# A transformer block on one core: what the last token tile of each batch does before attention starts, and where two small pieces of work stand

## Chip, cores and metric

The kernel runs on one core of one Trainium2 chip. Its time is in device microseconds; the figure for a kernel is the median of its runs. The kernel before has three runs: 3191.1, 3191.3 and 3192.64 us, so its median is 3191.3 us. One more execution was profiled. All times of instructions come from that one execution and count from the start of its span.

## The reference, cut to what matters

The block takes two sequences of 2048 tokens with 576 features (B = 2, N = 2048, C = 576, 16 heads of 36 features).

```
mod = silu(c) @ w_ada + b_ada                       # six rows of 576 per batch
xn  = layernorm(x) * (1 + sc_msa) + sh_msa
q, k, v = split((xn @ w_qkv + b_qkv) by head)       # 576 -> 1728
q = layernorm(q per head) * qn_g + qn_b
k = layernorm(k per head) * kn_g + kn_b
o = softmax(q @ k.T * 36**-0.5) @ v                 # per batch and head, 2048 x 2048 scores
x = x + g_msa * (o @ w_proj + b_proj)
h = gelu((layernorm(x) * (1 + sc_mlp) + sh_mlp) @ w1 + b1)   # 576 -> 2304
x = x + g_mlp * (h @ w2 + b2)                       # 2304 -> 576
```

All tensors are float32.

## The kernel before

A branch on the size of the gains and biases picks `block_of_small`, the only branch of interest. It goes through six stages in this order: for batch 0 the products q, k, v (`inputs`), attention (`attend`) and the output projection (`outputs`); the same three for batch 1; then the first product of the MLP for eight blocks of 512 tokens, and the second product.

**`inputs`.** The tokens of a batch are cut into 16 tiles of 128 (t = 0 to 15). For each tile TensorE makes three products (`product`, L1085 for the four full chunks of features and L1087 for the last 64). Each fills one tile of PSUM named `s`, two banks large, of which there are four in rotation. DVE adds the bias on the way out of PSUM (`biased`: L1099 for q and k into `both`, L1102 for v into `vt`). Then, for q and k, ACT squares (`squared`), DVE sums the squares by head, ACT takes the root, DVE the reciprocal, and POOL multiplies (`head_scale`, L1043, L1046, L1048, L1050). `by_feature` (L1063, L1065) transposes a tile in squares of 32 on DVE into one of two buffers `turned_qk`, and four DMAs on SP's queue store it by feature in a tensor `qk` in DRAM. Rows of one head pair are read back from there by `take_k_block` and `take_q` (L812, L814, SP's queue) for the first head pair, and by `take_k` (POOL's queue) for the other seven. The 36 features of a head are split: 32 go to `km` or `qm`, 4 to `ke` or `qe`, each of these four repeated. The rows then get their gain and bias on DVE and the four last features are split into two parts of a product in float32r (`scaled`, `parted`: L843 twice, L852, L853). For a block of key rows these four DVE instructions are the function `made` that `take_k_block` returns.

`key_tiles` lists where the key rows of the first head pair are cut into blocks: after tiles 4, 8, 12, 14 and 16. When `by_feature` has stored the tile that ends a block, it issues that block's loads and puts `made` in the list `taken`; the next call of `by_feature` with `ready=True` runs what is in the list, after its own transpose and stores. What is left in the list at the end of the stage is handed to attention, which runs it in its second step (hook (0, 0, 0) puts it in front of the list for step 1).

The loop over t from 0 to 14 has the same order for every tile; the last tile, t = 15, has its own sequence, which is what most of the change is about. Once in batch 0 `gains_by_row` turns gains and biases into one number per row of `km`, `ke`, `qm`, `qe` (`gb_at`): DVE fills two selection matrices (L824, L829), TensorE multiplies them with the gains (L835), DVE copies the result out (L838). `kept` stores the prepared weights in DRAM for batch 1. Both are called in the iteration t = 2.

**`attend`.** A step is one head pair, one block of 512 queries and a quarter of the keys. TensorE makes the scores of the step (`scores`, L1203, eight banks of PSUM), ACT takes exponentials (L1207), and in the next step TensorE multiplies the exponentials of the step before with v (`values`, L1216), and DVE adds the result to `ot` (L1264, L1266). The column range of `km` that a step reads is a quarter g of its 1024 columns; its rows 0 to 63 hold tokens 0 to 1023 and rows 64 to 127 tokens 1024 to 2047. So step g = 2 reads tiles 4, 5, 12 and 13, and step g = 3 reads 6, 7, 14 and 15. The eight banks `b` lie where the four tiles `s` of `inputs` were, and a bank can be written once the `s` tile in its place has left PSUM.

**The first product of the MLP.** 144 jobs alternate between two sets of banks. A job has its matmuls (L1625, L1639) and then `gelu_stored`: ACT copies one bank (L1651), DVE combines seven products into four (L1652 to L1659), ACT takes gelu (L1663). Beside them `ahead` prepares the next block of tokens, tile by tile: load from `x1_dram` (`mlp_loaded`, POOL's queue), normalise and transpose on DVE (`tile_turned`), store, read back, modulate on ACT. The first two loads, for tiles 1 and 2 of block 1, are issued before the first job, ahead of `token_sums(0)` in the text of the program.

**What sets the order.** PE runs in the order of the text throughout, and DVE in the order of the text in all stages that matter here; in attention ACT and POOL do too. The order of the other queues is set by a scheduler, from what it takes each instruction to wait for. It had put the two first loads of the MLP, which need only rows of batch 0, into POOL's queue at the last tile of batch 1, between the multiplications of `head_scale`.

Of the kernel before, what the change touches and what calls it, by code (L numbers as in the profile page):

```python
# [31 lines left out]
def dit_block(  # L32
# [25 lines left out]
    nc = tc.nc  # L58
# [9 lines left out]
    TPB = BLK // P  # L68
# [54 lines left out]
    def halves(ap):  # L123
        return ap.rearrange("p (a f) -> p a f", a=2)
# [627 lines left out]
    def block_of_small():  # L752
# [3 lines left out]
        xs = {}  # L756
# [114 lines left out]
        def take_k_block(t0, t1):  # L871

            c, k0 = divmod(t0 * P, N // 2)
            dst, rows = slice(k0, k0 + (t1 - t0) * P), slice(64 * c, 64 * c + 64)
            rows_taken(nc.sync, km[0], ke[0], (c,), C, lambda c: slice(t0 * P, t1 * P), dst)

            def made():
                scaled(km[0][rows, dst], km[0][rows, dst], rows, 1)
                parted(ke[0][:, dst], rows, 1)

            return made

        def take_q(p, qb):
            i, full = qb % 2, slice(0, P)
            src = lambda c: slice(qb * BLK, (qb + 1) * BLK)
            rows_taken(nc.sync, qm[i], qe[i], range(2), p * 2 * HD, src, slice(0, BLK))
            return [lambda: scaled(qm[i], qm[i], full, 0), lambda: parted(qe[i], full, 0)]
# [140 lines left out]
        def inputs(b, weights, making, work, xnts, turned, loaded):  # L1028

            wq, wq4, bq = weights  # L1030
            both, squares, taken = {}, {}, []
            key_tiles = (0, 4, 8, 12, 14, 16)

            def squared(t, w0=0, w1=2):
                if squares.get("t") != t:
                    squares.update(t=t, sq=work.tile([P, 2 * C], F32, name="sq", bufs=1))
                part = slice(w0 * C, w1 * C)
                nc.scalar.activation(squares["sq"][:, part], both[t][:, part], AF.Square)

            def head_scale(t, w0=0, w1=2):  # L1040
                n, part = (w1 - w0) * H, slice(w0 * C, w1 * C)
                var = work.tile([P, 2 * H], F32, name="var", bufs=2)[:, :n]
                nc.vector.tensor_reduce(  # L1043
                    var, squares["sq"][:, part].rearrange("p (h d) -> p h d", d=HD), AX.X, ALU.add
                )
                nc.scalar.activation(var, var, AF.Sqrt, bias=eps5, scale=1.0 / HD)  # L1046
                inv = work.tile([P, 2 * H], F32, name="inv", bufs=2)[:, :n]
                nc.vector.reciprocal(inv, var)  # L1048
                heads = both[t][:, part].rearrange("p (h d) -> p h d", d=HD)
                nc.gpsimd.tensor_tensor(heads, heads, inv.unsqueeze(2).to_broadcast([P, n, HD]), ALU.mult)  # L1050
# [5 lines left out]
            def by_feature(t, w0=0, w1=2, ready=True):  # L1056

                begun = [*taken] if ready else []
                if ready:
                    taken.clear()  # L1060
                part = slice(w0 * C, w1 * C)
                turned_qk = work.tile([P, 2 * C], F32, name="turned_qk", bufs=2)
                nc.vector.transpose(turned_qk[:, part], both[t][:, part])  # L1063
                for g in range(P // SQ):
                    nc.sync.dma_start(  # L1065
                        out=by_square[t, g][:, w0 * NSQ : w1 * NSQ, :],
                        in_=turned_qk[g * SQ : (g + 1) * SQ, part].rearrange("p (k j) -> p k j", j=SQ),
                    )
                for do in begun:
                    do()  # L1070
                if t == TPB - 1 and w0 == 0:
                    taken.extend(take_q(0, 0))
                if t + 1 in key_tiles and w1 == 2:
                    i = key_tiles.index(t + 1)
                    taken.append(take_k_block(*key_tiles[i - 1 : i + 1]))
# [18 lines left out]
            def biased(w, ps, t):  # L1094
                bias = halves(bq[:, w * C : (w + 1) * C])
                if w < 2:
                    if t not in both:
                        both[t] = work.tile([P, 2 * C], F32, name="both", bufs=4)
                    nc.vector.tensor_tensor(halves(both[t][:, w * C : (w + 1) * C]), ps[:, :, :HALF], bias, ALU.add)  # L1099
                else:  # L1100
                    heads = "p a (h d) -> p a h d"
                    nc.vector.tensor_tensor(  # L1102
                        vv[:, t, :, 0:HD].rearrange("p (a h) d -> p a h d", a=2),
                        ps[:, :, :HALF].rearrange(heads, d=HD),
                        bias.rearrange(heads, d=HD),
                        ALU.add,
                    )
# [37 lines left out]
            for t in range(NT - 1):  # L1145
                begun(t)
                if t >= done:
                    q = product(0, t)
                k = product(1, t)
                if t >= done:  # L1150
                    biased(0, q, t)
                turned_ahead(t)
                biased(1, k, t)
                if t > 0:
                    head_scale(t - 1)
                if t >= done:
                    v = product(2, t)
                    biased(2, v, t)
                if b == 0 and t == 2:
                    gains_by_row(work)  # L1160
                    kept()
                if t >= 2:
                    by_feature(t - 2)
                squared(t)
                modulated_ahead(t)

            t = NT - 1
# [2 lines left out]
            by_feature(t - 2)  # L1170
            biased(1, k, t)
            squared(t, 1, 2)
            by_feature(t - 1)
            head_scale(t, 1, 2)
            by_feature(t, 1, 2)
            biased(0, q, t)
            squared(t, 0, 1)
            biased(2, v, t)
            head_scale(t, 0, 1)
            by_feature(t, 0, 1, ready=False)  # L1180
# [359 lines left out]
        for j in range(TPB + 1):  # L1540
            n, t = divmod(j, TPB)
# [15 lines left out]
        def mlp_loaded(n, i, queue):  # L1557
            b, blk = divmod(n, NBLK)
            t0 = blk * BLK + i * P
            return tile_loaded(x1_dram[b, t0 : t0 + P, :], queue)  # L1560
# [31 lines left out]
        def token_sums(n):  # L1592
            a = xnts[n % 2][0]
            a00, a01, a10, a11 = (a[:, 2 * k : 2 * k + 2, t * PAIR : (t + 1) * PAIR] for t in range(2) for k in range(2))
            nc.vector.tensor_tensor(ss[1], a10, a11, ALU.add)
            nc.vector.tensor_tensor(ss[2], ss[1], a00, ALU.subtract)
            nc.vector.tensor_tensor(a10, a00, a10, ALU.subtract)
            nc.vector.tensor_tensor(ss[4], a01, ss[2], ALU.subtract)
# [107 lines left out]
            nc.sync.dma_start(out=hidden[q % len(hidden)], in_=gelus[n][g])  # L1706

        rows_ahead = {}
        for i in (1, 2):
            rows_ahead[1, i] = mlp_loaded(1, i, nc.gpsimd)  # L1710
        token_sums(0)
        for job in range(0, NB * HF, 2):
            (n0, f0), (n1, f1) = divmod(job, HF), divmod(job + 1, HF)
            ahead(job)
# [157 lines left out]
```

## Time and profile before

| what | value |
|---|---|
| median of the three runs | 3191.3 us |
| the profiled execution: its own time | 3187.14 us |
| its span, first to last instruction | 3185.4 us |
| TensorE busy | 3122.8 us, 98% of the span |
| DVE, ACT, POOL busy | 48%, 46%, 21% |
| mean granted TensorE clock | 0.992 |

The profile lists for each engine when it was busy, and for the time before an instruction in which its engine was idle, what released it ("<-"). TensorE's matmuls are pipelined and their ends are modelled. An idle engine costs time only where the engine that sets the end waits for it. Here that is TensorE almost everywhere: between 2193 and 2690 us, the middle of the first MLP product, it is busy for 497.00 of 497.00 us.

### The profile page before, as it was taken

The page shows a single profiled execution, that of the slowest core. Times are in us where ns is not written, and L with a number is a line of the kernel's source. Part 1 is how long each engine was busy: PE and PEld are TensorE (multiplying, and loading weights), DVE is VectorE, ACT ScalarE, POOL GpSimd, SP SyncE. Part 2 cuts the span into 40 slices and gives each one's busy share as a digit, 9 for nine tenths or more (in the row PEclk, how much of TensorE's full clock was granted, in tenths as well). Part 3 has the DMA queues.
Part 4 walks back from the last instruction along what each step waited for, and adds up shares of the span by engine and source line. Part 5 has one row for each costly group of instructions (what it writes and reads, how often), then busy time and mean ns, then how long its engine had stood idle before and what let it go on. Part 6 is the DMA issues. An engine that isn't in the chain of part 4 may idle for free.

```text
span 3185.4 us, 46758 instructions
## 1 busy us (share of the span) xinstructions
PE 3122.8 (98%) x17553; PEld 1865.6 (59%) x17553; DVE 1518.5 (48%) x2182; ACT 1471.6 (46%) x2843; POOL 658.1 (21%) x921
## 2 busy tenths in 40 slices
PE   7998999999999999899999999999999999999999
PEld 5873333333333787633333333358888888777777
DVE  6653344433434555434434444346566554455454
ACT  2225666666666122266666666642555552000000
POOL 4551000111110455300001111113333320121121
PEclk9998999999999999899999999999999999999999
DMA  6554211222221756511122222246554433333331
GB/s 187 115 108 97 76 45 56 67 74 67 73 73 41 213 112 118 97 39 46 46 49 69 81 64 68 65 139 189 155 144 131 138 108 143 124 126 112 119 104 38
DMA packets 304454, 311.94 MB, mean 98 GB/s; under 512 B 183450, under 2 KB 237466, under 8 KB 302107
## 3 DMA queue, kind: packets, MB, share of 16 engines
q1 hardware_dynamic: 256834, 193.37, 21.2%
q0 software_dynamic: 43840, 109.88, 13.3%
q10 hardware_dynamic: 3544, 5.60, 0.5%
q8 instruction: 141, 2.31, 0.3%
q14 instruction: 95, 0.77, 0.1%
HBM read 191.79 MB, written 106.46 MB: 94 GB/s over the span
## 4 chain that ended last, share of the span: by engine, by line
PE 92%; DMA 2%; issue 2%; DVE 2%; POOL 1%; SPq 1%; ACT 0%; POOLq 0%; DVEq 0%
PE b L1216 29%; PE b L1203 19%; PE s L1784 15%; PE m L1625 12%; PE s L1085 9%; PE s L406 2%; PE m L1639 2%; PE one L1625 2%; PE s L1087 1%; POOL turned L988 1%; POOL both L1050 1%; DMA xt<-in_x_dram 0%; DMA x_dram<-spare 0%; PE s L417 0%; DVE turned_qk L1063 0%
## 5 line engine op out<-in xcount | busy, mean ns | idle before, releaser
L1207 ACT ACTIVATE pt<-b 128x512 f32<-128x512 f32 x2048 | 1057.2, 608 | 478.3 <-PE b L1216 271.8
L1216 PE MATMUL b<-pt,vt 128*64 128x512 f32 x4096 | 935.0, 598 | 0.0
L1216 PEld LDWEIGHTS b<-pt,vt 128*64 128x64 f32 x4096 | 271.8, 136 | 582.1 <-issue 438.8
L1203 PE MATMUL b<-qm,km 32*128 32x512 f32 x4096 | 568.9, 618 | 28.6 <-DVE both L1099 28.6
L1266 DVE TENSOR_TENSOR ot<-b,ot 128x512 f32<-128x512 f32 x192 | 132.7, 691 | 620.4 <-PE b L1216 620.4
L1203 PE MATMUL b<-qe,ke 16*128 16x512 f32 x2048 | 425.0, 797 | 0.0
L1085 PE MATMUL s<-wq,xnt 128*128 128x288 f32 x1536 | 405.7, 407 | 2.5 <-ACT xnt L395 2.1
L1203 PEld LDWEIGHTS b<-qm,km 32*128 32x128 f32 x4096 | 193.8, 186 | 299.5 <-ACT pt L1207 209.7
L1784 PE MATMUL s<-ws,as 128*128 128x288 f32 x1440 | 351.8, 406 | 0.0
L1085 PEld LDWEIGHTS s<-wq,xnt 128*128 128x128 f32 x1536 | 281.4, 190 | 65.0 <-ACT xnt L395 1.6
L1784 PEld LDWEIGHTS s<-ws,as 128*128 128x128 f32 x1440 | 273.6, 190 | 75.6
L1235 DVE RECIPROCAL den<-den 128x512 f32<-128x512 f32 x64 | 213.6, 3337 | 10.0 <-DMA den<-den_dram 10.0
L1625 PE MATMUL m<-xnt,wb 128*128 128x256 f32 x864 | 210.2, 379 | 0.9 <-issue 0.9
L1625 PE MATMUL m<-s,wb 128*128 128x256 f32 x864 | 210.0, 379 | 0.0
L988 POOL DMA_DIRECT2D turned<-squares x212 | 142.9, 680 | 285.2 <-DVE squares L983 268.2
L1264 DVE COPY ot<-b 128x512 f32<-128x512 f32 x64 | 44.3, 691 | 282.2 <-PE b L1216 282.2
L1625 PEld LDWEIGHTS m<-s,wb 128*128 128x128 f32 x864 | 164.2, 190 | 22.3
L1203 PEld LDWEIGHTS b<-qe,ke 16*128 16x128 f32 x2048 | 109.3, 185 | 114.5 <-issue 113.7
L1625 PEld LDWEIGHTS m<-xnt,wb 128*128 128x128 f32 x864 | 158.9, 190 | 20.3 <-issue 1.3
L1663 ACT ACTIVATE cs<-cs,b_sb 128x512 f32<-128x512 f32 x144 | 98.9, 719 | 114.5 <-DVE cs L1658 92.5
L812 POOL DMA_DIRECT2D km<-qk x56 | 27.9, 499 | 571.4 <-PE b L1203 568.9
L1784 PE MATMUL s<-ws,hidden 128*128 128x288 f32 x576 | 142.3, 406 | 0.0
(199 smaller groups left out, 2897.2 us busy)
## 6 DMA issues: line engine op xcount, KB each, us to landing
gelu<-cs SPq DMA_DIRECT2D x144, 256.0 KB
hidden<-gelu SPq DMA_DIRECT2D x16, 2304.0 KB
x_dram<-spare POOLq DMA_DIRECT2D x64, 288.0 KB, 2.5
qk<-turned_qk SPq DMA_DIRECT2D x120, 144.0 KB
qm<-qk SPq DMA_DIRECT2D x256, 64.0 KB
den<-den_dram SPq DMA_DIRECT2D x128, 128.0 KB
turned<-squares POOLq DMA_DIRECT2D x212, 72.0 KB, 2.5
xnt<-turned POOLq DMA_DIRECT2D x54, 256.0 KB, 4.0
```

The costliest lines, as they stand in the source:

```text
L406: nc.tensor.matmul(outs[a], stationary(k, a), moving(k, a), start=(first and k == 0), stop=(not first and k == FULL - 1),)
L988: queue.dma_start(out=by_square[g], in_=squares[g * SQ : (g + 1) * SQ, :].rearrange("p (k j) -> p k j", j=SQ))
L1085: nc.tensor.matmul(out_a, full[:, k, :], wq[:, k, f], start=k == 0, stop=False)
L1203: nc.tensor.matmul(ps, k[r, keys], q[r, :], start=first, stop=not first)
L1207: nc.scalar.activation(pt[:, h, :], banks[2 * c + h], AF.Exp, scale=SCALE)
L1216: nc.tensor.matmul(acc[64 * h : 64 * h + 64, :], vt[:, v0 : v0 + 64], pt[:, h, :], start=pt is pts[0][0], stop=pt is pts[-1][0],)
L1235: nc.vector.reciprocal(den, den)
L1266: nc.vector.tensor_tensor(ot, acc, ot, ALU.add)
L1625: nc.tensor.matmul(out_m[m], wb[:, slot[m], k, f * P : (f + 1) * P], moving[m](k), start=k == 0 and m in (1, 2, 5, 6), stop=k == 1 and m == 1,
L1639: nc.tensor.matmul(out_m[m], wr[w][:, f * P : (f + 1) * P], a[:, i, t * PAIR : (t + 1) * PAIR], start=False, stop=i == 1 and m != 2,)
L1663: nc.scalar.activation(part, part, AF.Gelu, bias=b1_sb[:, g : g + 1])
L1784: nc.tensor.matmul(ms[m], stationary[m][:, f, :], ws[m][:, f, :], start=(f == 0), stop=(f == HF - 1))
```

## The change

Four edits, in three places.

1. `key_tiles` loses its entry 14. The key rows of tiles 12 to 15 become one block of 512 columns; its loads are issued when tile 15's k rows have been stored, and its four DVE instructions run in attention's second step. Before, tiles 12 and 13 were a block of their own, made within `inputs`.
2. In the last tile's sequence, `head_scale` for k moves ahead of the transpose of tile 14, q leaves PSUM ahead of the transpose of tile 15's k rows, and v directly after that transpose.
3. `gains_by_row` and `kept` move from iteration t = 2 to t = 5 (`TPB` is 4).
4. `token_sums(0)` goes ahead of the two first loads of the MLP, and DVE writes one element of each load's tile before it, so the load follows that write.

```
-            key_tiles = (0, 4, 8, 12, 14, 16)
+            key_tiles = (0, 4, 8, 12, 16)
...
-                if b == 0 and t == 2:
+                if b == 0 and t == TPB + 1:
                     gains_by_row(work)
                     kept()
...
             by_feature(t - 2)
             biased(1, k, t)
             squared(t, 1, 2)
+            head_scale(t, 1, 2)
             by_feature(t - 1)
-            head_scale(t, 1, 2)
-            by_feature(t, 1, 2)
             biased(0, q, t)
             squared(t, 0, 1)
+            by_feature(t, 1, 2)
             biased(2, v, t)
             head_scale(t, 0, 1)
             by_feature(t, 0, 1, ready=False)
...
         rows_ahead = {}
+        token_sums(0)
         for i in (1, 2):
+            nc.vector.memset(xs["tiles"][0][0:1, 0:1], 0.0)
             rows_ahead[1, i] = mlp_loaded(1, i, nc.gpsimd)
-        token_sums(0)
```

In the built program the scheduler also moves other things. POOL's queue no longer has the two loads in batch 1's last tile; they stand after the last stores of batch 1's `outputs`. On SP's queue the loads for tiles 12 and 13 are gone, and the loads for tiles 12 to 15 stand where those for 14 and 15 stood, behind the first store of tile 15's q rows. The three stores of `kept` keep their place on SP's queue, near its start. On ACT's and POOL's queues one modulation each changes places with a neighbour (at about the seventh tile, and ACT's also at the first MLP jobs).

More of the change, by code (lines that the diff above doesn't have):

```diff
@@ L1031, in inputs @@
             both, squares, taken = {}, {}, []
-            key_tiles = (0, 4, 8, 12, 14, 16)
+            key_tiles = (0, 4, 8, 12, 16)
             def squared(t, w0=0, w1=2):
@@ L1158, in inputs @@
                     biased(2, v, t)
-                if b == 0 and t == 2:
+                if b == 0 and t == TPB + 1:
                     gains_by_row(work)
@@ L1172, in inputs @@
             squared(t, 1, 2)
+            head_scale(t, 1, 2)
             by_feature(t - 1)
-            head_scale(t, 1, 2)
-            by_feature(t, 1, 2)
             biased(0, q, t)
             squared(t, 0, 1)
+            by_feature(t, 1, 2)
             biased(2, v, t)
@@ L1708, in block_of_small @@
         rows_ahead = {}
+        token_sums(0)
         for i in (1, 2):
+            nc.vector.memset(xs["tiles"][0][0:1, 0:1], 0.0)
             rows_ahead[1, i] = mlp_loaded(1, i, nc.gpsimd)
-        token_sums(0)
         for job in range(0, NB * HF, 2):
```

## The prediction

> **What bounds the kernel now.** I read the page's first part, then TensorE's own waits, and around each wait the timelines of the other engines.
>
> ```profile
> PE 3122.8 (98%) x17553; PEld 1865.6 (59%) x17553; DVE 1518.5 (48%) x2182; ACT 1471.6 (46%) x2843; POOL 658.1 (21%) x921
> PE b L1203 <- DVE both L1099: 28.6, 2, 14.4
> PE s L835 <- issue: 9.1, 1, 9.1
> ```
>
> TensorE sets the end: busy 98% of the span. An edit is worth what it does to TensorE's gaps. After the start there are three of note: two of about 14.3 us, one per batch, before attention's scores (the columns are total, count, longest), and one of 9.1 us before the matmul L835 of `gains_by_row`. The change touches all three. First the 14.4 us of batch 0, DVE's timeline:
>
> ```profile
> 247.84 0.72 DVE L1099 TENSOR_TENSOR both<-s,bq 128x576 f32<-128x576 f32 x1
> 248.67 1.38 DVE L1063 STREAM_TRANSPOSE turned_qk<-both 128x1152 f32<-128x1152 f32 x1
> 256.89 0.42 DVE L843 TENSOR_SCALAR km<-km,gb_at 64x256 f32<-64x256 f32 x1 [6.85 <-DMA km<-qk]
> ...
> 259.07 0.75 DVE L1043 TENSOR_REDUCE var<-sq 128x16 f32<-128x576 f32 x1
> 261.79 0.78 DVE L1063 STREAM_TRANSPOSE turned_qk<-both 128x576 f32<-128x576 f32 x1 [1.33 <-POOL both L1050]
> 262.49 0.72 DVE L1099 TENSOR_TENSOR both<-s,bq 128x576 f32<-128x576 f32 x1
> 275.45 0.69 DVE L1264 COPY ot<-b 128x512 f32<-128x512 f32 x1 [8.06 <-PE b L1216]
> ```
>
> TensorE's last product ended at 248.89. DVE took out tile 15's k, turned tile 14, then stood 6.85 us before the split of tiles 12 and 13, whose rows were still on their way through DRAM. Only at 262.49 did q leave PSUM; TensorE's first score follows at 263.26. After it ACT sets the pace: its table load for the exponential waits in order behind the root for q, and the first `values` start at 271.72.
>
> ```profile
> 265.07 1.28 ACT L1207 ACT_TABLE_LOAD   x1
> 266.36 5.00 ACT L1207 ACTIVATE pt<-b 128x512 f32<-128x512 f32 x10
> 254.01 0.31 SPq L812 DMA_DIRECT2D km<-qk  x1
> 1327.32 1.12 POOL L967 DMA_DIRECT2D xt<-x_dram  x2 [13.12 <-PE s L1087]
> ```
>
> The third line gives a DMA time: tile 13's stores begin at 247.94, and the load that needs them goes at 254.01, so stores land about 6.1 us after the first is issued. The last line is batch 1: the two MLP loads wait on POOL until 1326.8 for TensorE, and tile 14's multiplication behind them runs at 1328.46, though its factor was ready at 1324.24. There TensorE gets three first scores in at 1326.69, then waits to 1342.01 for q.
>
> **Edits 1 and 2, batch 0.** DVE in the new order, with the durations above: k out at 248.56; square on ACT to 249.33; sum 0.75, root 0.31, reciprocal 0.25 with their hand-overs to 250.78; transpose of tile 14 to 252.16 (its factors were multiplied by 248.64); q out by 252.85. So the first score comes at 252.9 instead of 263.26. The transpose of tile 15's k rows must wait for tile 13's stores, which read the same one of two buffers: 254.0 to 254.8. v leaves at 255.45; TensorE needs its banks in its second block of scores, at about 255.2, so this hides. Sum for q to 256.25, root to 256.6, table load to 257.9: exponentials start at 257.9, not 266.36, and with the 5.36 us that lay between these and `values` before, `values` starts at 263.3, not 271.72: 8.4 us earlier. The earlier q alone would have given 10.4; the buffer wait and the root keep 2.
>
> The split then costs. Before, the block needed at step g = 2 was made in `inputs` and hidden. Now DVE makes it after the copy of `ot`, which waits for the end of `values` (3.6 us): 266.9. Copy 0.69, then the four instructions at 512 columns: the block of tiles 8 to 11 took 241.73 to 244.24, 2.51 us with a short DMA wait in it; I take 2.35. `km` is ready at 268.2 and `ke` at 270.0. TensorE would go on at 266.75 with the scores of g = 2; it does the first four banks' `km` part at 268.25 and the `ke` part at 270.05, and then 0.64 and 1.2 us to the next `values`: 271.9, against 269.1 without a stall. Price 2.75 us. Queued behind it on DVE are the scalings of the next q block, needed two steps later. Net: 277.69 becomes 271.9, **5.8 us**.
>
> This holds if the rows have landed. On SP tile 14's stores follow at 252.2 and land by 258.3 (6.1 us); tile 15's k rows, half the size, go at 254.85 and land at about 260. The loads stand behind the first store of q rows: sum to 256.25, multiplied to 258.15, turned to 259.2, store 259.7. So loads go at 260 and take the 4.0 us from first issue to last landing that tiles 8 to 11 took (238.32 to 242.36): 264.0, against 267.6 when DVE asks. Cover 3.6 us; beyond it every microsecond is lost once per batch. The loads for the next q block move behind them to about 264 to 271, and are first needed by DVE at 270.
>
> **Batch 1.** Here edit 4 takes the MLP loads out of POOL's queue, so tile 14 is multiplied at 1324.3. By the same steps q leaves at 1330.4, tile 13's stores land at 1331.6, v is out at 1333.05, the exponentials start at 1335.5 against 1345.12: 9.9 us with a little less half-speed work. Less 2.75: **7.1 us**. Without edit 4, tile 14's multiplication would end at 1330.6 and some 2 us of this be lost.
>
> **Edit 3.** At t = 2 it looks like 9 us to be had. But TensorE's next product needs tile 3's modulated input, and this is late for another reason:
>
> ```profile
> 72.50 0.15 DVE L824 COPY sel<-ident 32x128 f32<-32x128 f32 x1
> ...
> 73.16 1.63 ACT L1005 ACTIVATE xnt<-xnt,mod 128x128 f32<-128x128 f32 x4
> 76.89 0.46 POOL L390 TENSOR_TENSOR xnt<-tail,xnt 128x128 fp32r<-128x128 f32 x1
> ...
> 115.36 0.76 DVE L1102 TENSOR_TENSOR vt<-s,bq 128x576 f32<-128x576 f32 x1 [1.65 <-PE s L1087]
> ```
>
> ACT modulates it at 73.16 behind a root that DVE's sum at 70.51 releases, all ahead of `gains_by_row`, and the product's last chunk waits for POOL at 76.89 (it went at 77.57). So the removal gives 0.0 to 0.2 us: I take 0. At t = 5 TensorE is not held by anything (v ended at 115.32, q of tile 6 followed at once). Now L835 stands between: DVE frees v at 116.03, fills the two matrices in 0.58 (0.15 + 0.40 and a hand-over), L835 goes at 116.7 and takes 0.7 to 1.0 (0.98 at half speed before). The product starts at 117.4: **2.1 us lost**, bounds 1.3 and 2.5. A matmul wait at 171.37 (1.06 us, on POOL) might absorb up to 1.06; I don't count on it. `kept` keeps its place and costs nothing; the two swaps on ACT and POOL push one DVE reciprocal by about 1.6 us against DVE idle times of 1.65 and 2.37 us there: 0.
>
> **Edit 4, at the MLP.** The loads now follow `token_sums(0)`:
>
> ```profile
> 2189.39 0.81 DVE L272 BATCH_NORM_STATS2 st<-xt 128x6 f32<-128x288 f32 x2
> ...
> 2192.98 0.69 DVE L1652 TENSOR_TENSOR cs<-m,cs 128x512 f32<-128x512 f32 x1 [0.59 <-PE m L1639]
> xt<-x_dram POOLq DMA_DIRECT2D x3, 288.0 KB, 3.3
> ```
>
> The two writes of one element are about 0.1 us each (nearest row: 0.11 us for a 1x11 memset on POOL). The load goes at about 2189.7 and lands 3.0 to 5.2 us later (that tile's range here), since two weight loads are filling the DMA engines. So `bn_stats` moves from 2189.39 to 2193 to 2195, and `gelu_stored` of job 0, queued behind 3 us of it, ends at 2198.9 to 2200.8 instead of 2195.6. Job 2 writes these banks from 2199.78, bank by bank. So it is hidden by 0.9 us or just not: 0, worst 3; I take 0.2.
>
> **The sum**: 5.8 + 7.1 - 2.1 - 0.2 = 10.6 us. The profiled execution took 3187.14 (span 3185.4 and 1.7 around it), 4.2 under the median of the runs; a difference carries over, so 3191.3 - 10.6 = **3180.7 us**.
>
> **A rule that speaks against it.** After the 9.05 us gap the first product took 3.88 us where it takes 2.10; after the 1.06 us gap at 171.37 the next took 2.10. Between the two the trace is silent. The Trainium skill (TensorE: Matmul & The Clock Gate, section Why this matters for your kernels) says that an idle stretch above some 3 us sends the clock back to half. The new stalls are 1.3 us at t = 5 and, at g = 2, 1.5 and 1.2 us apart with matmuls between: by the rule they stay warm, and I take that. If they did count, each would cost about 1.8 us more (3.88 - 2.10): three of them make 5.4, and 3186.1. The gap of 4.0 us that is left before the first score is above the bound, so these scores start at half speed, as before; ACT hides that.
>
> **The rivals.** (a) The clock falls in the new stalls, or the split's stall is longer by that much: 3186.1. For it: the stalls are new and close together; against: the rule. (b) Slower: the rows of tiles 12 to 15 land late, on SP's queue behind the q store. From 267.6 each microsecond costs 2 in all; it eats the whole gain at 5.3 us later, 272.9, and landing at 277.5, as late against the first score as twice the estimate, gives 3200. For it: 128-byte stores that land 6.1 us after issue, more of them in a row than before; against: 3.6 us of cover. (c) The MLP rows come 3 to 6 us later than the worst row: 3185 to 3187. (d) The change doesn't do it: something else holds the first score till the old time. The first score's wait ends 0.05 us after q left in both batches, so little: 3193 with edit 3's loss. (e) More gain: the buffer wait isn't there and TensorE absorbs the rest: up to 3175.
>
> **How the numbers follow.** Forecast 0.62, (a) 0.13, (b) 0.07, (c) 0.06, (d) 0.04, (e) 0.08. About 0.2%, 6.4 us, is what a measurement of this kernel tells from no change, so 3184.9 and 3197.7 are the bounds. Faster: forecast, (e) and a part of (a) and (c): 0.74; slower: (b) and a little, 0.08; within: 0.18. The range 3174.5 to 3188.5 leaves out (b), (d) and tails; the forecast's own is 3177 to 3184.
>
> **What would show it.** First scores at about 253 and 1330.5; exponentials at about 258 and 1335.5; a TensorE wait on DVE's L843 and L853 in attention's third step of some 2.75 us, twice; the 9 us wait at t = 2 still there, now on ACT's modulation; a wait of 1.3 us before L835 near 116.7. Wrong if DVE waits for a DMA before the split (b), or if the gap at t = 2 closes.

## The result

| kernel | median, us | runs | ratio to before, 95% interval |
|---|---|---|---|
| before | 3191.46 (3188.78 to 3193.54) | 13 | |
| changed | 3184.31 (3182.12 to 3186.1) | 13 | 0.9977 [0.9969, 0.9986] |

The change takes 7.15 us off, 0.22%. The forecast was 10.6 us and 3180.7 us: the sign is right, the time lies in the range, the gain is two thirds of the forecast, and the median lies just above the 3177 to 3184 us that the forecast gave as its own. The profiled execution of the changed kernel took 3184.77 us, its span 3182.9 us. That span is only 2.5 us shorter than the profiled one of before; why the runs show 7.15 is part of what had to be found out.

Busy times of the changed kernel's engines, and the waits of its TensorE; a line of waits gives the total, the count and the longest in us:

```profile
PE 3133.2 (98%) x17553; PEld 1868.5 (59%) x17553; DVE 1517.7 (48%) x2176; ACT 1471.4 (46%) x2843; POOL 655.0 (21%) x921
```

```profile
PE s L1085 <- ACT xnt L1005: 10.1, 1, 10.1
...
PE b L1203 <- DVE both L1099: 6.3, 2, 3.9
...
PE s L835 <- issue: 2.0, 1, 2.0
PE b L1203 <- DVE vt L1102: 1.4, 1, 1.4
PE b L1203 <- ACT pt L1207: 1.4, 2, 1.0
PE m L1625 <- DVE cs L1659: 1.2, 1, 1.2
PE b L1203 <- DVE ke L853: 1.0, 2, 0.5
```

The two waits for q fell from 28.6 us together to 6.3. The wait at t = 2 is still there and has a new name, ACT's modulation. The others shown are new: 2.0 us before L835 at t = 5, 1.2 us in the MLP's third job, and some 4 us inside attention's first steps, where TensorE waits for v, for the exponentials and for the split. In all TensorE idles 49.7 us instead of 62.6, 12.9 less, but is busy 10.4 us longer with the same 17553 matmuls. That is the first sign that matmuls ran slower.

The order on DVE in batch 0, where TensorE's last product now ends at 253.43:

```profile
255.23 1.38 DVE L1063 STREAM_TRANSPOSE turned_qk<-both 128x1152 f32<-128x1152 f32 x1
256.53 0.72 DVE L1099 TENSOR_TENSOR both<-s,bq 128x576 f32<-128x576 f32 x1
258.32 0.78 DVE L1063 STREAM_TRANSPOSE turned_qk<-both 128x576 f32<-128x576 f32 x1 [1.07 <-DMA qk<-turned_qk]
...
273.58 0.69 DVE L1264 COPY ot<-b 128x512 f32<-128x512 f32 x1 [9.91 <-PE b L1216]
274.31 0.55 DVE L843 TENSOR_SCALAR km<-km,gb_at 64x512 f32<-64x512 f32 x1
```

And what ACT and TensorE make of it:

```profile
260.75 1.28 ACT L1207 ACT_TABLE_LOAD   x1
262.05 5.15 ACT L1207 ACTIVATE pt<-b 128x512 f32<-128x512 f32 x10
...
257.31 1.88 PE L1203 MATMUL b<-qm,km 32*128 32x512 f32 x6 [3.87 <-DVE both L1099]
268.56 4.95 PE L1216 MATMUL b<-pt,vt 128*64 128x512 f32 x16
276.69 0.50 PE L1203 MATMUL b<-qe,ke 16*128 16x512 f32 x2 [0.50 <-DVE ke L853]
278.20 3.65 PE L1216 MATMUL b<-pt,vt 128*64 128x512 f32 x16
```

q leaves PSUM, the k rows of tile 15 wait 1.07 us for tile 13's stores, the exponentials start 8.62 us after the last product; the forecast's 257.9 was 9.0 after its 248.89. All that came as worked out. But the first `values` take 4.95 us instead of 3.65.

### The profile page after: what moved, and what is told of

It is laid out like the page before. It is cut to its first block, busy times and chain, and to the rows that moved or that the text cites. A ratio compares the mean times of both kernels' runs of the same rounds, so it can differ in the third digit from the quotient of the medians.

```text
span 3182.9 us, 46730 instructions
## 1 busy us (share of the span) xinstructions
PE 3133.2 (98%) x17553; PEld 1868.5 (59%) x17553; DVE 1517.7 (48%) x2176; ACT 1471.4 (46%) x2843; POOL 655.0 (21%) x921
## 4 chain that ended last, share of the span: by engine, by line
PE 90%; DVE 3%; DMA 2%; issue 1%; POOL 1%; SPq 1%; ACT 0%; DVEq 0%; POOLq 0%; ACTq 0%
PE b L1216 29%; PE b L1203 19%; PE s L1785 15%; PE m L1625 11%; PE s L1085 7%; PE s L406 2%; PE m L1639 2%; PE one L1625 2%; PE s L1087 1%; POOL turned L988 1%; POOL both L1050 0%; DMA bq<-in_b_qkv_dram 0%; DMA xnt<-turned 0%; PE s L417 0%; DVE turned_qk L1063 0%
## 5 line engine op out<-in xcount | busy, mean ns | idle before, releaser
L1085 PE MATMUL s<-wq,xnt 128*128 128x288 f32 x1536 | 407.1, 408 | 12.5 <-ACT xnt L1005 10.1
L1085 PEld LDWEIGHTS s<-wq,xnt 128*128 128x128 f32 x1536 | 282.3, 191 | 75.8 <-ACT xnt L1005 10.3
L1005 ACT ACTIVATE xnt<-xnt,mod 128x128 f32<-128x128 f32 x244 | 100.3, 481 | 101.8 <-DMA xnt<-turned 95.3
## 6 DMA issues: line engine op xcount, KB each, us to landing
gelu<-cs SPq DMA_DIRECT2D x144, 256.0 KB
xnt<-turned POOLq DMA_DIRECT2D x54, 256.0 KB, 4.0
```

The costliest lines, as they stand in the source:

```text
L1005: nc.scalar.activation(part, part, AF.Identity, **affine(which, k, b))
L1085: nc.tensor.matmul(out_a, full[:, k, :], wq[:, k, f], start=k == 0, stop=False)
```

## Where the clock stood

From here on times within a batch are counted from the end of its last product. "Second values" is the start of the second row of `values`; two such rows are 5.98 us apart when nothing holds TensorE. A line of the profile's table by stretches of time gives the stretch and its length, the busy time of TensorE's matmuls, TensorE's weight loads, DVE, ACT and POOL, and then, as the third number from the end, the clock granted to TensorE: 1.00 is full speed, 0.50 half. First the kernel before, then the changed one:

```profile
252.00:254.00 2.00, 0.00 (x0) 0.00 (x0) 0.00 (x0) 0.00 (x0) 0.00 (x0) 0.50 0.94 134
...
266.00:268.00 2.00, 2.00 (x15) 1.37 (x10) 0.78 (x1) 1.99 (x5) 2.00 (x4) 0.50 0.10 9
268.00:270.00 2.00, 2.00 (x18) 1.37 (x15) 0.00 (x0) 2.00 (x5) 2.00 (x5) 0.94 0.71 143
```

```profile
258.00:260.00 2.00, 2.00 (x16) 1.61 (x13) 1.68 (x3) 0.00 (x0) 0.00 (x0) 0.50 1.02 185
...
262.00:264.00 2.00, 1.30 (x5) 0.88 (x6) 0.78 (x1) 1.99 (x6) 1.90 (x4) 1.00 1.01 150
...
268.00:270.00 2.00, 2.00 (x7) 0.53 (x6) 0.00 (x0) 0.00 (x0) 0.82 (x3) 0.50 0.99 196
```

Before, the clock halved while TensorE idled (PE busy 0.00) and was back at 268, ahead of the first `values` at 271.72. The half clock fell into the gap and cost nearly nothing. In the changed kernel the gap is 3.9 us; the same kind of phase now lies on the scores. The clock is back at full speed for some 3.5 us, and then a second phase, from 264.5, covers the first `values`.

Read in stretches of 0.5 us, the half-clock phases around the start of attention, with the stages they weigh on ("products" is batch 0, first product to last; MLP is the first job's start to the fourth job's L1639):

| kernel | products | half clock, batch 0 | second values, batch 0 | half clock, batch 1 | second values, batch 1 | MLP |
|---|---|---|---|---|---|---|
| before | 229.61 | 251.0 to 268.0 | 28.80 | 1330.0 to 1350.5 | 30.29 | 26.93 |
| before again | 230.87 | 253.5 to 270.5 | 28.62 | 1335.5 to 1359.5 | 33.22 | 26.93 |
| edit 3 | 232.41 | 256.0 to 269.5 | 28.80 | 1334.5 to 1358.5 | 33.23 | 26.93 |
| edit 4 | 229.67 | 251.0 to 268.0 | 28.74 | 1333.0 to 1350.0 | 29.19 | 28.43 |
| edits 1, 2 | 230.64 | 253.5 to 270.5 | 25.81 | 1332.0 to 1342.0 | 25.12 | 26.93 |
| edit 1 | 231.39 | 254.5 to 261.0 | 23.43 | 1329.5 to 1343.0 | 26.70 | 26.92 |
| edits 1, 2, 4 | 231.39 | 254.0 to 264.5 | 22.78 | 1329.5 to 1343.0 | 25.50 | 28.32 |
| changed | 234.36 | 257.5 to 261.0, 264.5 to 271.0 | 24.77 | 1333.0 to 1346.5 | 25.32 | 28.39 |

"Edits 1, 2" and "edits 1, 2, 4" run the same instructions up to here in batch 0, and differ by 3.03 us, with a half clock of 17 and of 10.5 us. So a single profile of these kernels is known to some 3 us per batch only. The Trainium skill (TensorE: Matmul & The Clock Gate, section Part 1: The HAM clock gate) says that the clock is set by a free-running window of about 3.4 us, so that a slow phase varies from run to run, and that one busy window ends it. The lengths here, about 3.5, 7, 10, 13.5, 17, 20.5 and 24 us, do look like whole windows. That one busy window ends it these runs don't show: with edits 1 and 2 the profile has TensorE busy for 1.6 to 2.0 of every 2 us from 256 to 270, at half clock throughout. What the clock counts as busy no run here shows.

This also settles the 2.5 against 7.15 us. The profiled execution of before was 4.3 us below the median of the runs; the second one, of the same kernel, has 2.93 us more in batch 1, 1.26 more in the products and 2.05 more in the projection after attention. The changed kernel's is 0.5 us above its own median. 7.15 - 4.3 - 0.5 is 2.4.

## The experiments

**The kernel before, again.** Unchanged.

> The kernel before, unchanged, for a second profile. The two profiled executions differ by 2.5 us of span (3185.4 and 3182.9), while the medians of 13 runs each differ by 7.15 us. Theory: the profiled execution of before was an unusually quick one, and a second one has a span of about 3189 to 3190, with one stage visibly longer than in the first (a product or a score run at half clock for longer after a gap). Rival: its span is again 3185.4 and the difference lies outside the span. The ratio of the times is 1 within its interval.

3190.96 us (11 runs), ratio 0.9996 [0.9987, 1.0005]. This is the row "before again" above.

**Edits 1 and 2 alone.**

```
-            key_tiles = (0, 4, 8, 12, 14, 16)
+            key_tiles = (0, 4, 8, 12, 16)
...
-            by_feature(t - 1)
             head_scale(t, 1, 2)
-            by_feature(t, 1, 2)
+            by_feature(t - 1)
             biased(0, q, t)
             squared(t, 0, 1)
+            by_feature(t, 1, 2)
```

> Edits 1 and 2 alone (one block for tiles 12 to 15, new order of the last tile). Theory from the two traces: about 4 us gained in batch 0 (277.69 to 273.7 us for the second values, after taking off the 4.5 us that edit 3 costs ahead of it) and 4 in batch 1, where the two MLP loads still hold POOL; together 8 us, ratio 0.9975. Rival, as forecast: 5.8 and 5 us, 0.9966.

3180.55 us (5 runs), 0.9965 [0.9951, 0.9978]: 11.75 under the 3192.3 us of before beside it. The forecast's terms without edit 4's help are 5.8 + 7.1 - 2 = 10.9. The interval holds this and the theory's 8 us alike; the median is nearer to the first. The whole gain is here; the median has more of it than the changed kernel keeps, though the intervals overlap.

**Edit 3 alone.**

```
-                if b == 0 and t == 2:
+                if b == 0 and t == TPB + 1:
                     gains_by_row(work)
```

> Edit 3 alone (factors by row at the sixth tile). Theory: the 9 us gap before tile 3's product stays, since ACT's modulation ends it, and TensorE loses 4.7 us at the sixth tile: some 2.2 of waiting, 0.9 for the small matmuls, 1.5 for a product at half clock; ratio 1.0015. Rival, as forecast: 2.1 us lost, 1.0007.

3192.43 us (11 runs), 1.0005 [0.9996, 1.0014]: the runs don't tell it from no change, and the theory's 1.0015 lies just outside the interval. Its timeline at t = 5, DVE then TensorE:

```profile
116.25 0.37 DVE L824 COPY sel<-ident 32x128 f32<-32x128 f32 x1
...
116.73 0.80 PE L835 MATMUL s<-gb_rows,sel 128*128 128x4 f32 x4 [1.19 <-issue]
117.39 2.19 PE L1085 MATMUL s<-wq,xnt 128*128 128x288 f32 x8
```

The product before began its L1087 at 114.90 and the next would have followed 0.48 us on, at 115.38: 2.0 us lost, 2.1 forecast. The changed kernel at the same place:

```profile
115.81 1.22 DVE L824 COPY sel<-ident 32x128 f32<-32x128 f32 x1
...
117.14 0.35 PE L835 MATMUL s<-gb_rows,sel 128*128 128x4 f32 x2 [2.04 <-issue]
117.68 0.59 PE L835 MATMUL s<-gb_rows,sel 128*128 128x4 f32 x2 [0.19 <-DVE sel L829]
118.13 3.61 PE L1085 MATMUL s<-wq,xnt 128*128 128x288 f32 x8
```

The same copy takes 1.22 us; POOL's multiplication for the tile before ran from 114.84 to 116.96 and the copy ended as it did, 117.03; with edit 3 alone that multiplication was over when the copy began. 1.2 us more are lost, and then the product runs at half clock (0.50 in the table by stretches from 118 to 121), 1.5 us more. Together 4.7 us, which is what its products stage has over before's 229.61; over the 231.39 of two other kernels without edit 3 it is 3.0.

**Edit 4 alone.**

```
+        token_sums(0)
         for i in (1, 2):
+            nc.vector.memset(xs["tiles"][0][0:1, 0:1], 0.0)
             rows_ahead[1, i] = mlp_loaded(1, i, nc.gpsimd)
-        token_sums(0)
```

> Edit 4 alone (loads after the sums). Theory: TensorE waits 1.2 to 1.5 us for DVE before job 2 of the MLP, and batch 1's gap before the first scores is shorter by about 1.5 us since POOL multiplies tile 14 on time; together no change, ratio 1.0000. Rival: the early loads cost nothing in the old order, since DVE waits for the rows of tiles 12 and 13 anyway; then 1.5 us are lost, 1.0005.

3189.43 us (11 runs), 0.9991 [0.9982, 1.0]. At the MLP it costs 1.50 us by the table, and in batch 1 it wins 1.1 us against the quick execution of before and 4.0 against the others. The changed kernel shows the cost:

```profile
2185.33 0.06 DVE L1711 MEMSET xt<- 1x1 f32 x2
2191.48 0.84 DVE L272 BATCH_NORM_STATS2 st<-xt 128x6 f32<-128x288 f32 x2 [6.08 <-DMA xt<-x_dram]
...
2197.05 1.99 PE L1625 MATMUL m<-xnt,wb 128*128 128x256 f32 x8 [1.21 <-DVE cs L1659]
```

POOL issued the load at 2185.71 and DVE could use it 5.77 us later. `gelu_stored` of the first job stands behind it, and the third job waits for that job's banks.

**Edit 1 alone**: one block for tiles 12 to 15, the last tile's sequence as before.

```
-            key_tiles = (0, 4, 8, 12, 14, 16)
+            key_tiles = (0, 4, 8, 12, 16)
```

> Edit 1 alone: the keys of tiles 12 to 15 are taken as one block, the last tile's order of work is as before. Theory (the split that stood in VectorE's queue ahead of the last tile's q and v was the whole delay, and edit 2 merely lets q pass one k transpose of about 1 us): q of tile 15 leaves PSUM about 1 us later than with edits 1 and 2 (first score near 254 instead of 253 us after the shift of the trace), but ScalarE still loads its table and starts its exponentials within about 1 us, so the time is 3181 to 3183, against 3180.6 with both. Rival (the order of edit 2 carries the gain, because q waits behind the transpose that waits for tile 13's stores): the first score moves by less than half, and the time is 3185 to 3189.

3181.52 us (8 runs), 0.997 [0.9959, 0.9981], 9.6 under the 3191.11 us of before beside it. The time is the theory's. The first score is 2.7 us later than with edit 2, though, and not 1: it comes 6.61 us after the products, because q now stands behind the transpose that waits for tile 13's stores:

```profile
255.95 0.78 DVE L1063 STREAM_TRANSPOSE turned_qk<-both 128x576 f32<-128x576 f32 x1 [2.70 <-DMA qk<-turned_qk]
256.65 0.72 DVE L1099 TENSOR_TENSOR both<-s,bq 128x576 f32<-128x576 f32 x1
```

Yet the exponentials start at 9.72 against 8.60 to 8.66 with edit 2, and second values at 23.43 against 22.78 to 25.81. So edit 1 carries nearly all; edit 2 moves the first score by 2.7 us and what sets the pace by 1.1.

**Edits 1, 2 and 4**: the changed kernel without edit 3.

```
-                if b == 0 and t == TPB + 1:
+                if b == 0 and t == 2:
                     gains_by_row(work)
```

> Edits 1, 2 and 4, without edit 3 (that is, the changed kernel with the factors by row made at the third tile again). Theory (edits add up; edit 3 costs 3.0 to 4.7 us at the sixth tile, edit 4 costs 1.5 us at the start of the MLP and gives nothing in batch 1 once the tail is shorter): 3180 to 3182, some 3 us under the changed kernel's 3184.3 and 1 to 1.5 us over edits 1 and 2 alone; the stretch from the MLP's first matmul is 1.5 us longer than before. Rival (edit 4 gives its 2 us in batch 1 as predicted): 3178 to 3179.

3180.84 us (6 runs), 0.9965 [0.9952, 0.9977], 10.27 under before. The changed kernel is 7.15 under, so in its place edit 3 costs 3.1 us; the two intervals overlap, but the traces say the same (231.39 against 234.36). Edit 4 on top of 1 and 2 makes no difference that the runs can tell (10.27 against 11.75). What it does to POOL in batch 1 is seen by comparing with edits 1 and 2; first these two alone, then with edit 4:

```profile
1327.03 1.13 POOL L967 DMA_DIRECT2D xt<-x_dram  x2 [13.12 <-PE s L1087]
1328.17 3.24 POOL L1050 TENSOR_TENSOR both<-both,inv 128x1152 f32<-128x1152 f32 x2
```

```profile
1321.52 2.13 POOL L1050 TENSOR_TENSOR both<-both,inv 128x1152 f32<-128x1152 f32 x1 [10.18 <-DVE inv L1048]
1325.60 1.15 POOL L1050 TENSOR_TENSOR both<-both,inv 128x576 f32<-128x576 f32 x1 [1.95 <-DVE inv L1048]
```

With the loads gone, the multiplication of tile 14 starts before the last product ends (1323.91) and not 1.7 us after it (1326.47). The exponentials start at 8.64 instead of 10.71: the 2 us of the forecast are there. They are gone again at the second values, 25.50 against 25.12: the half clock lasted to 19.1 us after the products in the one and 15.5 in the other, and the first `values` took 5.51 us against 3.65.

**The split ahead of attention's first copy**, on edits 1 and 2: what is left in `taken` runs in attention's first step instead of the second, while DVE idles.

```
-                    later[1] = (hooks[p, qb, g]() or []) + later[1]
+                    i = 0 if behind is None else 1
+                    later[i] = (hooks[p, qb, g]() or []) + later[i]
```

> Edits 1 and 2, and the split of the last key rows put ahead of the copy of attention's first sums on VectorE instead of behind it. Theory (the 2.3 to 2.8 us that TensorE waits in attention's third step are owed to the split standing behind that copy, while VectorE was idle for 9.9 us before it): the rows have landed by about 268, the split is done by about 271, the wait in the third step is under 0.3 us in both batches, and the time is 3175 to 3177, 4 to 5.5 us under edits 1 and 2 alone. Rival (the rows land only after 272, or ScalarE's exponentials set the pace there anyway): the wait only changes its place and the time stays at 3179.5 to 3181.5.

3179.04 us (5 runs), 0.9964 [0.995, 0.9978], 12.07 under before: the runs don't separate it from edits 1 and 2 (11.75). TensorE's wait in the third step is gone in both batches (no wait above 0.45 us), and second values follow the first 7.85 us later in batch 0, first `values` at half clock included (8.36 at full clock in the kernel with edits 1, 2 and 4). Counted from the products, second values are at 23.05 and 25.07, no sooner than the best of the kernels without the early split (22.78 and 23.15); half clock lasted to 20.9 us after the products in batch 1. DVE's and SP's timelines show the reason for the little that it gives:

```profile
261.51 0.31 SPq L812 DMA_DIRECT2D km<-qk  x1
...
265.42 0.55 DVE L843 TENSOR_SCALAR km<-km,gb_at 64x512 f32<-64x512 f32 x1 [6.01 <-DMA km<-qk]
267.35 0.55 DVE L843 TENSOR_SCALAR ended<-ke,gb_at 64x512 f32<-64x512 f32 x1 [1.38 <-DMA ke<-qk]
...
270.18 0.69 DVE L1264 COPY ot<-b 128x512 f32<-128x512 f32 x1 [0.97 <-PE b L1216]
```

DVE now waits for the rows. The last of them is there 17.97 us after the products (ended at 249.38), the split is done at 19.83. The forecast had 15.1 for the landing and wanted them at 18.7: of the 3.6 us of cover 0.7 were real. The loads went out at 12.1 instead of 11.1 and took 5.8 us instead of 4.0.

**The same with eight more matmuls**, which fill the gap ahead of the scores; nobody reads their sums.

```
             k, q, v = (product(w, t) for w in (1, 0, 2))
+            warm = s_tile()
+            for i in range(2 * FULL):
+                nc.tensor.matmul(
+                    warm[:, i % 2, :HALF],
+                    xnts[t][0][:, i // 2, :],
+                    wq[:, i // 2, (i % 2) * HALF : (i % 2 + 1) * HALF],
+                    start=i < 2,
+                    stop=i >= 2 * FULL - 2,
+                )
```

> As the kernel before it in this call (edits 1 and 2, split ahead of the first copy), and eight more matmuls of 288 columns, whose sums nobody reads, behind the last tile's products, into the 3.9 us in which TensorE waits for q to leave. Theory (the half clock in attention's first steps is what the gap ahead of the scores leaves): granted clock 1.00 through the first two steps, first values x16 at 3.65 us instead of 4.95 to 5.4, 1.3 to 2 us per batch, 2.5 to 4 us in all. Rival (the scores then run earlier at full clock and wait longer for the exponentials, and the clock falls in that wait instead): the half clock moves by 2 to 4 us, the first values stay above 4.5 us, and the time is within 1 us of the kernel without the extra matmuls, or 1 us longer because the extra sums keep a PSUM bank.

3178.83 us (6 runs), 0.9963 [0.9951, 0.9976]: no difference. The half clock came later and shorter in batch 0 (260.5 to 263.5), and the first `values` ran at 3.65 us there, as the theory said; but then TensorE waits 1.03 us for the split. Batch 1 still has 13.5 us of half clock from 1332.0, and its first `values` take 5.86 us. Second values: 22.39 and 25.72.

**The two selection matrices of edit 3 early**: `gains_by_row` is split in two, so that the copies are made at the third tile as before (`sels_made`) and only the 4-column matmuls and the eviction stay at the sixth; otherwise the changed kernel. The split itself is not shown.

```
+                if b == 0 and t == 2:
+                    sels_made(work)
                 if b == 0 and t == TPB + 1:
-                    gains_by_row(work)
+                    gains_by_row()
                     kept()
```

> The changed kernel, but the two matrices that spread the factors (the copies on L824 and L829) are made at the third tile again, where VectorE idles, and only their product with the factors and its eviction stay at the sixth. Theory (edit 3 costs its 2 to 3.2 us gap because TensorE waits for those copies, one of which ran beside a multiplication of GpSimd, and in some executions a half clock after it): the wait before the 4-column matmuls is under 0.3 us, the next product runs at 2.10 us, the products of batch 0 take 230 to 231.5 us instead of 234.4, and the time is 3181 to 3182.5, against 3184.3. Rival (the wait is for something else at that place, the PSUM tile or the factors' rows): wait of 1 us or more as before, 3183.5 to 3185.

3182.1 us (9 runs), 0.9973 [0.9963, 0.9983], 9.7 under before where the changed kernel is 7.15 under; the two intervals overlap. The products take 230.64 us, as without edit 3. TensorE at t = 5 (L839 and L1089 are L835 and L1085 in this kernel):

```profile
116.11 0.50 PE L839 MATMUL s<-gb_rows,sel 128*128 128x4 f32 x4
116.47 2.19 PE L1089 MATMUL s<-wq,xnt 128*128 128x288 f32 x8
```

No wait, and the next product at full clock: the cost of edit 3 was the wait for DVE's copies, with what the clock made of it. In its batch 0 a half clock of 17 us still covers the first `values` (5.57 us, second values at 25.51). Its batch 1 shows the clock once more: half clock is over at 1341.0, the first `values` at 1341.74 take 3.65 us, and the second come at 23.15, where the forecast had 30.29 - 7.1 = 23.2.

**The changed kernel with twelve more matmuls** (as above with `3 * FULL`, some 6 us), so that TensorE has work until the exponentials start.

> The changed kernel, with twelve more matmuls of 288 columns (sums that nobody reads, some 6 us at full clock) behind the last tile's products in each batch, so that TensorE has work until the exponentials can start. Theory (the 3.5 us that the prediction has too much are the half clock that follows TensorE's gap): granted clock 1.00 up to the first values, these x16 at 3.65 us in both batches, second values 22.5 to 23.2 us after the end of the products in batch 0 and 22.8 to 23.5 in batch 1, instead of 24.8 and 25.3; time 3180 to 3182. Rival (the clock falls again while TensorE waits for the exponentials, whatever ran before): second values within 0.7 us of the changed kernel's, time 3183.5 to 3185.5.

3185.89 us (11 runs), 0.9981 [0.9972, 0.999]: 5.9 under before, no gain over the changed kernel, and second values at 25.17 and 24.86 after the products, as the rival said. The theory that the gap ahead of the scores causes the half clock, and that filling it would bring the 3.5 us, fell:

```profile
262.00:264.00 2.00, 1.19 (x11) 0.58 (x4) 0.67 (x1) 1.99 (x4) 2.00 (x4) 1.00 0.98 184
264.00:266.00 2.00, 2.00 (x14) 1.17 (x12) 0.11 (x1) 2.00 (x6) 0.41 (x1) 1.00 0.97 174
266.00:268.00 2.00, 2.00 (x12) 1.65 (x8) 0.00 (x0) 1.56 (x4) 0.50 (x2) 0.50 0.20 44
```

```profile
269.06 5.50 PE L1225 MATMUL b<-pt,vt 128*64 128x512 f32 x16
```

The clock stayed at 1.00 through the whole old gap and fell at 266.0, with TensorE busy in every stretch (1.19 us of 2 in the lowest, its longest wait 0.81 us), for 7 us, on the first `values` (L1225 here). In batch 1 it fell at 1341.0, for 7 us too. What these two phases have in common is that TensorE works in short bursts behind ACT's exponentials; that this causes them was not tried by itself.

The same run shows a half clock at t = 5 once more:

```profile
117.68 0.36 PE L835 MATMUL s<-gb_rows,sel 128*128 128x4 f32 x2 [1.26 <-issue]
...
118.47 3.47 PE L1085 MATMUL s<-wq,xnt 128*128 128x288 f32 x8
```

TensorE waited 1.26 us here, hardly longer than the 1.19 us with edit 3 alone, after which the product took 2.19 us.

**A better version**: edits 1 and 2, the early split, and of edit 4 the two marks alone, with `token_sums(0)` left behind the loads.

```
         for i in (1, 2):
+            nc.vector.memset(xs["tiles"][0][0:1, 0:1], 0.0)
             rows_ahead[1, i] = mlp_loaded(1, i, nc.gpsimd)
         token_sums(0)
```

> Edits 1 and 2, the split ahead of attention's first copy, and of edit 4 only the marks that hold the MLP's row loads back; the loads stay ahead of the token sums. Theory (the marks let batch 1's q leave some 2 us sooner, as the traces of all kernels with edit 4 show, and the 1.5 us at the MLP's start come from issuing the loads behind the token sums): k of tile 14 is transposed 1.5 us instead of 3.9 us after batch 1's products, the MLP's first stretch is back at 27.0 us, and the time is 3177 to 3178.5. Rival (the key rows' landing sets attention's third step, so that an earlier q gives nothing): 3179 to 3180.

3176.97 us (5 runs), 0.9956 [0.9943, 0.997]: 14.9 under before, the best time of all medians here. Edit 4's gain in batch 1 is kept (exponentials at 8.73, second values at 22.89), but its cost at the MLP falls only from 1.46 to 0.90 us. The theory had expected 0.1:

```profile
2174.33 0.06 DVE L1711 MEMSET xt<- 1x1 f32 x2
...
2182.49 0.82 DVE L272 BATCH_NORM_STATS2 st<-xt 128x6 f32<-128x288 f32 x2 [5.55 <-DMA xt<-x_dram]
...
2188.03 1.99 PE L1626 MATMUL m<-xnt,wb 128*128 128x256 f32 x8 [0.65 <-DVE cs L1660]
```

Counted from the first token sum (2174.33 here, 2182.77 in the changed kernel) POOL issues the load 2.05 us sooner, at 2175.22; but it is 7.3 us until DVE can use it, instead of 5.8.

**That version with the twelve matmuls.**

> As the kernel before it in this call, with the twelve extra matmuls behind the last tile's products. Theory (full clock and early split add up): second values 20.5 to 22.5 us after the end of the products in both batches, 3175 to 3177. Rival (the last key rows land only 17 to 19 us after the products, and TensorE waits for the split instead of running slowly): second values no sooner than 22 us, a wait of 0.5 to 1.5 us on the split in the third step, and the time within 1 us of the kernel without the extra matmuls.

3177.36 us (5 runs, 3174.06 to 3181.04), 0.9962 [0.9948, 0.9976]. Its profiled execution had no half clock in either batch, second values at 21.50 and 22.24 with a wait of 0.58 and 1.32 us on the split, and the shortest span of all, 3172.3 us. Its mean granted clock was 0.998; the other four runs had 0.996 or 0.997 and were slower, and the median is the same as without the extra matmuls.

## Why the prediction was right and where it failed

The forecast's sum beside the changed kernel's profile, with the profile of before that the forecast was made from:

| term | forecast, us | measured, us | at the clock assumed |
|---|---|---|---|
| edits 1, 2, batch 0 | -5.8 | 24.77 - 28.80 = -4.03 | -6.02 (edits 1, 2, 4: 22.78) |
| edits 1, 2, 4, batch 1 | -7.1 | 25.32 - 30.29 = -4.97 | -7.14 (edit 3 with early matrices: 23.15) |
| edit 3 | +2.1 | 234.36 - 229.61 = +4.75 | +2.0 (edit 3 alone) |
| edit 4 at the MLP | +0.2 | 28.39 - 26.93 = +1.46 | |
| sum | -10.6 | -2.79 (spans: -2.5) | |

The column on the right has the same term from the kernel named, where the clock was full over the first `values`, or at t = 5.

**Edits 1 and 2: the mechanism right, step by step.** DVE's order, the wait of the k transpose for tile 13's stores, the table load and the start of the exponentials came within 0.4 us. The price of the split, 2.75 us, is 2.4 where the clock was full (8.36 between first and second values, less 5.98); TensorE's waits on L853 show only 0.5 us each time, because the banks' first parts go on in between. The step that failed is "so these scores start at half speed, as before; ACT hides that". The half clock does not stay on the scores. Before, most of it passed while TensorE idled, though in batch 1 two of the four profiles with the old order had it on the first `values` too (5.48 and 5.62 us). In the changed kernel it covers the first `values` of both batches, in batch 0 by the second phase, and nothing hides that: 24.77 against 22.78 and 25.32 against 23.15 in kernels that run the same instructions there, 2.0 and 2.2 us. What starts a phase stays open: the matmuls that filled the gap did not remove it.

One reading was off without cost: v's way out of PSUM does not quite hide in batch 1, where TensorE waits 1.4 us for it (L1102 in the list of waits), but the exponentials start at 8.57 there as in batch 0.

**Rival (a)** was the right mechanism with a wrong place: not only in the new stalls, and one that comes and goes. It named 3186.1; the median is 3184.31. The rule that the forecast took, that idle stretches under some 3 us stay warm, did not hold at t = 5: after 2.04 us and four 4-column matmuls a product ran at half clock, in the kernel with twelve more matmuls after 1.26 us. With edit 3 alone the clock stayed up after 1.19 us, so the length of the wait does not decide it by itself.

**Edit 3.** The gap was sized right for the quiet case. Left out was that the DVE copy may meet an instruction on POOL: 0.15 us in the row that the forecast used, 0.37, 0.45 and 1.22 at t = 5 in three kernels, ending each time 0.07 to 0.08 us after a multiplication on POOL (L1050, or L390 behind it). That the removal at t = 2 gives nothing came as said.

**Edit 4.** "Hidden by 0.9 us or just not", taken as 0.2, was the mis-sized term: 1.46, with a load that took 5.77 us from issue to use, beyond the 3.0 to 5.2 of the rows used. That is far from rival (c), which had it 3 to 6 us beyond them. The 2 us that it brings in batch 1 were found at the exponentials and were lost to the clock after them.

**Rival (b)** did not happen: in the changed kernel the split begins 20.9 us after the products (274.31), with no wait for the rows, and the early split had them at 17.97. But against the 18.7 at which the forecast had the split begin, the cover was 0.7 us and not 3.6; the half clock, which delays the split, made it wider. Rivals (d) and (e) are out: the first score came when q left, and nothing more was gained.

**The base.** "A difference carries over" failed as well, in the other direction: the profiled execution of before was quick by 2.9 us in batch 1 because its half clock lasted 20.5 us there and not 24. The change removes that very stretch, so the usual execution gains more than the profiled one. Against the second profile of before the terms are 3.85 + 7.90 - 3.49 - 1.46 = 6.8 us, and the runs show 7.15. (These two spans differ by 9.3 us; 2.05 of the rest lie in the projection after attention, which the change does not touch.) That the time lies well inside the stated range is thus in part luck: the forecast carried over from the one profile, with the terms as they came out there, would have been 3191.3 - 2.8 = 3188.5, the edge of the range.

## What to carry to other kernels

A gap on TensorE hides more than itself: while it lasts, a half-clock phase costs nothing. Shorten the gap and the phase can fall on the work: here a gap of 14 us cut to 4 gave 2 to 3 us less in the executions in which the phase lay on the first `values`. An insertion into a stretch where TensorE is full costs its wait and then possibly a product at half clock; put everything but the matmul itself where another wait covers it, as the matrices at the third tile. And before a difference of 3 us between two profiles is believed, profile the unchanged kernel twice.

## What was not expected of the hardware

- Half-clock phases last 3.5 to 24 us, in steps of about 3.4, differ between executions of the same instructions, and can begin with TensorE busy: after ten stretches of 2 us in which it was busy for 2.00, but for one with 1.19.
- A 32x128 copy on DVE took 0.15, 0.37, 0.45 and 1.22 us; all but the first ended 0.07 to 0.08 us after a multiplication on POOL.
- A 288 KB row load took 5.8 us from issue to use at the MLP's start, and 7.3 us when it was issued a little sooner; the cause of the longer one was not looked for.
